# Gated layer's first state turned in 32x32 blocks and exchanged through DRAM; attention as attention @ (h @ W)

## The chip, the cores and the metric

The kernel runs on one core of one Trainium2 chip. The metric is the device time of one execution in microseconds (us). The kernel before was run three times: 3126.87 us is the median, 3125.3 and 3129.24 are the ends. One execution was also taken by the hardware profiler.

## The reference

128 graphs of 128 nodes with 256 features go through four layers, each with a residual: x = x + layer(relu(layernorm(x))). All data are float32. Layers 0 to 2 are graph attentions, cut to what matters here:

```python
Wh = h @ W                                   # (graph, node, 256)
e = (Wh @ a1)[:, :, None] + (Wh @ a2)[:, None, :]
e = jnp.where(e > 0, e, 0.2 * e)
attention = softmax(jnp.where(adj > 0, e, -9e15), axis=-1)
x = x + elu(attention @ Wh)                  # layer 2: times a node mask before elu
```

Layer 3 is a gated graph layer of three steps. Its state begins as h = relu(layernorm(x)). In each step the neighbours are summed, and a GRU cell takes the sum and the state:

```python
aggr = A.T @ (h @ weight[i])
gi, gh = aggr @ w_ih.T + b_ih, h @ w_hh.T + b_hh
r, z = sigmoid(i_r + h_r), sigmoid(i_z + h_z)
n = tanh(i_n + r * h_n)
h = (1 - z) * n + z * h
```

## The kernel before

Four graphs form a group, and 32 groups are worked on. A node is on a partition, so one tile of a group is 128 partitions by 4 graphs by 256 features (`xt`, `xn`, `hn`, `xo`). The GRU works on the transposed form: features on partitions, the 512 nodes of the group along the row, two tiles of 128 features each.

`load` (L67) brings x and the adjacency of a group. `stats` (L170) makes the mean and variance on DVE, and the reciprocal standard deviation `rs` with a power on GpSimd. `attention` (L200) is one attention layer of one group. `xn` is the relu of x minus the mean (ACT); `rs` is a positive number per node, so it is multiplied in later. The scores are not read from h @ W: `VA` holds W @ a1 and W @ a2 spread over all partitions, made once at the start (L84 to L106). DVE makes the first score as a dot product with an accumulator (`scr`, L212), GpSimd multiplies for the second (`pr`, L217) and ACT adds up (L221). TensorE spreads the second score over the partitions by a transpose (`e2`, L229). DVE and ACT make the softmax (`em`, `nmx`, `pe`, L235 to L252). Then TensorE transposes the attention (`atp`, L261), DVE multiplies by `rs` on the way out (`at`), TensorE multiplies it with `xn` (`ahp`, L272), the product is copied to `ah` by ACT and DVE, and TensorE multiplies it with W (`hp`, L285). The elu with the residual is done on ACT (`t`, L291) and DVE (L293, L294) in halves of two graphs, on a tile `xo` that GpSimd filled with x - 1 (L257).

`gat` (L299) runs the three attentions of a group and makes the GRU's first state `hn` (L317). `turned` (L185) transposes it: eight 128x128 transposes on TensorE into PSUM (`hTp`, L191) and two copies (`hT`, L195 and L197). `gru` (L324) does the three steps. Per step, 24 products of 512 columns (L344), four neighbour sums per feature half (`agp`, L361), and from the second step on transposes of the state (`hnp`, L335). At the end the result is added to x and stored.

PSUM has eight banks, given out by tag (L62): two to the attention ("gat"), four to the GRU ("gru"), two to neighbour sums and state transposes ("tr").

The program runs each group's attention two groups ahead of its GRU, and a scheduler of the framework sets the order of instructions on each engine when the kernel is built. Each engine then takes its instructions strictly in this order, and each waits for what it needs. In the order that results, the attention of group g + 1 lies between the GRU products of group g, and the order is the same from group to group in the middle of the run. SP's queue issues all DMAs.

An engine's matmul in float32 is two instructions in the profile.

Of the kernel before, what the change touches and what calls it, by code (L numbers as in the profile page):

```python
# [8 lines left out]
FT = mybir.dt.float32  # L9
I32 = mybir.dt.int32  # L10
AF = mybir.ActivationFunctionType
OP = mybir.AluOpType
AX = mybir.AxisListType

P = 128
# [6 lines left out]
def kernel(  # L22
# [24 lines left out]
    nc = tc.nc  # L47
    B, N, D = x.shape
    KD = D // P
    G = 4  # L50
    NG = B // G
    T = G * N
# [3 lines left out]
    const = ctx.enter_context(tc.tile_pool(name="const", bufs=1))  # L56
# [4 lines left out]
    psum = ctx.enter_context(tc.tile_pool(name="psum", bufs=1, space=bass.MemoryType.PSUM))  # L61
    BANKS = {"gat": 2, "gru": 4, "tr": 2}  # L62

    def bank(tag, name):
        return psum.tile([P, T], FT, tag=tag, name=name, bufs=BANKS[tag])

# [10 lines left out]
    ident = const.tile([P, P], FT, name="ident")  # L77
# [5 lines left out]

    W, VA = [], []  # L84
    for l, (w, a) in enumerate(((w0, a0), (w1, a1), (w2, a2))):
        wt = const.tile([P, KD, D], FT, name=f"w_{l}")
        nc.sync.dma_start(wt, w.rearrange("(k p) o -> p k o", p=P))
        ab = su.tile([P, 2, D], FT, tag="ab", name=f"ab_{l}")
        nc.sync.dma_start(ab, bass.AP(tensor=a.tensor, offset=a.offset, ap=[[0, P], [1, 2 * D]]))
        wa = su.tile([P, 2, KD], FT, tag="wa", name=f"wa_{l}")  # L90
        vp = bank("gat", f"vp_{l}")
        for s in range(2):
            for k in range(KD):
                scr = su.tile([P, D], FT, tag="scr", name=f"scr_{l}_{k}_{s}")
                nc.vector.scalar_tensor_tensor(
                    scr, wt[:, k, :], 1.0, ab[:, s, :], op0=OP.mult, op1=OP.mult,
                    accum_out=wa[:, s, k : k + 1],
                )
                c = s * KD + k
                nc.tensor.transpose(  # L100
                    vp[:, c * P : (c + 1) * P], wa[:, s, k : k + 1].to_broadcast([P, P]), ident
                )
        va = const.tile([P, 2, D], FT, name=f"va_{l}")
        nc.vector.tensor_copy(va.rearrange("p s d -> p (s d)"), vp)
        W.append(wt)
        VA.append(va)  # L106

# [57 lines left out]

    setup.close()
    rw = ctx.enter_context(tc.tile_pool(name="rw", bufs=2))

# [31 lines left out]
    def attention(g, l, xt, cap):  # L200
# [5 lines left out]
        for b in range(G):  # L206
            nc.scalar.activation(xn[:, b, :], xt[:, b, :], AF.Relu, bias=nm[:, b : b + 1])  # L207

        e = gw.tile([P, 2, G], FT, tag="e", name=f"e_{name}")
        for b in range(G):  # L210
            scr = gw.tile([P, D], FT, tag="scr", name=f"scr_{name}_{b}")
            nc.vector.scalar_tensor_tensor(  # L212
                scr, xn[:, b, :], rs[:, b : b + 1], VA[l][:, 0, :], op0=OP.mult, op1=OP.mult,
                accum_out=e[:, 0, b : b + 1],
            )
        pr = gw.tile([P, G, D], FT, tag="pr", name=f"pr_{name}")
        nc.gpsimd.tensor_tensor(  # L217
            pr, xn, VA[l][:, 1 : 2, :].to_broadcast([P, G, D]), op=OP.mult
        )
        for b in range(G):  # L220
            nc.scalar.activation(  # L221
                pr[:, b, :], pr[:, b, :], AF.Copy, scale=rs[:, b : b + 1],
                accum_out=e[:, 1, b : b + 1],
            )
        yield

        e2 = bank("gat", f"e2_{name}")
        for c in range(G):
            nc.tensor.transpose(  # L229
                e2[:, c * P : (c + 1) * P], e[:, 1, c : c + 1].to_broadcast([P, P]), ident  # L230
            )

        em = gw.tile([P, G, N], FT, tag="em", name=f"em_{name}")
        for c in range(G):
            nc.vector.scalar_tensor_tensor(  # L235
                em[:, c, :], e2[:, c * P : (c + 1) * P], e[:, 0, c : c + 1], cap[:, c, :],
                op0=OP.add, op1=OP.min,
            )
# [16 lines left out]

        xo = grp.tile([P, G, D], FT, tag=f"x{l + 1}", name=f"xo_{name}", bufs=3 if l == 2 else 2)
        nc.gpsimd.tensor_scalar(xo, xt, 1.0, -1.0, op0=OP.mult, op1=OP.add)  # L257
        yield
        atp = bank("gat", f"atp_{name}")
        for b in range(G):  # L260
            nc.tensor.transpose(atp[:, b * P : (b + 1) * P], pe[:, b, :], ident)  # L261
        at = gw.tile([P, T], FT, tag="at", name=f"at_{name}")
        nc.vector.tensor_tensor(
            at.rearrange("p (g i) -> p g i", g=G), atp.rearrange("p (g i) -> p g i", g=G),
            rs.rearrange("p (g o) -> p g o", o=1).to_broadcast([P, G, N]), op=OP.mult,
        )

        ah = gw.tile([P, KD, T], FT, tag="ah", name=f"ah_{name}")
        for k in range(KD):
            ps = bank("gat", f"ahp_{name}_{k}")  # L270
            for c in range(G):
                nc.tensor.matmul(  # L272
                    ps[:, c * P : (c + 1) * P], xn[:, c, k * P : (k + 1) * P],
                    at[:, c * P : (c + 1) * P], start=True, stop=True,
                )
            if k % 2 == 0:
                nc.scalar.copy(ah[:, k, :], ps)
            else:
                nc.vector.tensor_copy(ah[:, k, :], ps)  # L279
        for j in range(G // 2):  # L280
            hp = bank("gat", f"hp_{name}_{j}")
            for b in range(2):
                c = 2 * j + b
                for k in range(KD):
                    nc.tensor.matmul(  # L285
                        hp[:, b * D : (b + 1) * D], ah[:, k, c * P : (c + 1) * P], W[l][:, k, :],
                        start=(k == 0), stop=(k == KD - 1),
                    )

            t = gw.tile([P, T], FT, tag="t", name=f"t_{name}_{j}")  # L290
            nc.scalar.activation(t, hp, AF.Exp)  # L291
            u = xo[:, 2 * j : 2 * j + 2, :].rearrange("p b d -> p (b d)")
            nc.vector.scalar_tensor_tensor(u, hp, 0.0, u, op0=OP.max, op1=OP.add)  # L293
            nc.vector.scalar_tensor_tensor(u, t, 1.0, u, op0=OP.min, op1=OP.add)  # L294
        yield xo
# [3 lines left out]
    def gat(g):  # L299
# [16 lines left out]
        for b in range(G):  # L316
            nc.scalar.activation(  # L317
                hn[:, b, :], xt[:, b, :], AF.Relu, bias=nm[:, b : b + 1], scale=rs[:, b : b + 1]
            )
        hT = turned(hn, grp, "h0", f"{g}_3")  # L320
        done[g] = (xt, am, hn, hT)
        yield

    def gru(g):  # L324


        xt, am, hn0, h0 = done.pop(g)
        h = [h0[:, k, :] for k in range(KD)]
        hn = [[hn0[:, b, k * P : (k + 1) * P] for b in range(G)] for k in range(KD)]

        def node_major(i, k):
# [6 lines left out]
            return ps  # L338

        for i in range(STEPS):  # L340
            name = f"{g}_{i}"

            def mm(ps, c, w, v, k, start, stop):
                nc.tensor.matmul(  # L344
                    ps, w[:, k, c * P : (c + 1) * P], v[k], start=start, stop=stop
                )
# [22 lines left out]
            for c in range(KD):  # L369
# [34 lines left out]
                d = rw.tile([P, T], FT, tag="d", name=f"d_{name}_{c}")  # L404
                nc.vector.tensor_sub(d, h[c], n)
                nc.vector.scalar_tensor_tensor(d, z, 1.0, d, op0=OP.add, op1=OP.mult)
# [63 lines left out]
```

## Time and profile before

| what | value |
|---|---|
| median of three runs | 3126.87 us |
| profiled execution, time | 3126.87 us |
| profiled execution, span from first to last instruction | 3125.1 us |
| mean granted TensorE clock | 0.991 |
| TensorE busy before 160 us of the span (two stretches of 80) | 42.13 and 54.62 us |
| TensorE busy, 160 to 300 us | 134.00 of 140 us |
| DMA, share of 16 engines | 4.6% of the span in the one large queue |
| x of a group, 512 KB, issue to landing | 3.9 us |
| result of a group, 512 KB, issue to landing | 2.9 us |
| adjacency of a group, 256 KB | 2.7 us |

The span runs from the first instruction to the last; what lies around it in this execution is 1.8 us. In the first 120 us the weights are prepared and the attention of the first group runs alone, with nothing beside it; that is why TensorE is half idle there. In the lists of groups, a row has the line, the engine, the operation, the tiles and shapes and the count, then the busy time and mean duration of one, then the idle time of the engine just before such instructions, with what ended it. Mean durations of matmuls include their overlap with their neighbours. In a view in order of time, a bracket at the end gives the idle time before the row and what ended it.

### The profile page before, as it was taken

How to read it: one execution, taken by the hardware profiler on the slowest of the kernel's cores; microseconds unless marked ns; L12 is line 12 of the kernel's file. 1: busy time of each engine (PE TensorE's matmuls, PEld its weight loads, DVE VectorE, ACT ScalarE, POOL GpSimd, SP SyncE). 2: the span in 40 equal slices, each digit the busy share in tenths (PEclk: the TensorE clock that was granted, in tenths of full speed). 3: DMA queues.
4: the chain of work that ended last, by engine and by line, in shares of the span. 5: the costliest groups of instructions: out<-in, count | busy, mean ns of one | idle time of the engine just before them, and what ended most of it. 6: DMA issues, size and time to landing. Idle time of an engine off the chain costs nothing.

```text
span 3125.1 us, 32601 instructions
## 1 busy us (share of the span) xinstructions
PE 2941.1 (94%) x11105; PEld 1714.3 (55%) x11105; DVE 2163.8 (69%) x4731; ACT 1349.4 (43%) x3265; POOL 530.0 (17%) x454
## 2 busy tenths in 40 slices
PE   5699999999999999999999999999999999999999
PEld 3455555555555555555555555555555555555554
DVE  5667776767776777776777677677667677767663
ACT  1344444444444444444444444444444444444442
POOL 1212111212111212121112121112121121111110
PEclk8899999999999999999999999999999999999999
DMA  2000000000000000000000000000000000000000
GB/s 85 11 17 11 7 18 17 17 18 11 7 18 17 18 17 11 7 17 18 17 18 11 7 17 18 18 12 13 11 18 17 17 11 7 17 14 7 8 1 14
DMA packets 56199, 48.03 MB, mean 15 GB/s; under 512 B 3296, under 2 KB 55648, under 8 KB 56032
## 3 DMA queue, kind: packets, MB, share of 16 engines
q1 hardware_dynamic: 56032, 45.95, 4.6%
q8 instruction: 87, 1.43, 0.2%
q14 instruction: 80, 0.66, 0.1%
HBM read 29.17 MB, written 16.78 MB: 15 GB/s over the span
## 4 chain that ended last, share of the span: by engine, by line
PE 70%; DVE 13%; ACT 9%; POOL 6%; issue 1%; DMA 0%; ACTq 0%; SPq 0%; POOLq 0%; DVEq 0%
PE r L344 15%; PE z L344 15%; PE ni L344 9%; PE hp L285 7%; PE nn L344 7%; PE ahp L272 6%; POOL pr L217 5%; ACT xn L207 4%; PE agp L361 3%; DVE st L175 3%; DVE xo L294 3%; DVE xo L293 3%; ACT pr L221 2%; PE hnp L335 2%; PE e L229 2%; PE atp L261 2%
## 5 line engine op out<-in xcount | busy, mean ns | idle before, releaser
L212 DVE SCALAR_TENSOR_TENSOR scr<-xn,rs,va 128x256 f32<-128x256 f32 x384 | 386.0, 1053 | 73.0 <-POOL rs L182 71.1
L344 PE MATMUL r<-ag,wc 128*128 128x512 f32 x768 | 372.1, 593 | 0.0
L344 PE MATMUL ni<-ag,wc 128*128 128x512 f32 x768 | 371.4, 592 | 0.0
L285 PE MATMUL hp<-w,ah 128*128 128x256 f32 x1536 | 368.3, 383 | 0.7 <-DVE ah L279 0.7
L344 PE MATMUL z<-ag,wc 128*128 128x512 f32 x768 | 361.4, 592 | 0.0
L257 POOL TENSOR_SCALAR xo<-xo 128x1024 f32<-128x1024 f32 x64 | 67.5, 1055 | 1596.4 <-DVE mv L176 1596.4
L285 PEld LDWEIGHTS hp<-w,ah 128*128 128x128 f32 x1536 | 284.2, 190 | 76.8 <-DVE ah L279 26.3
L293 DVE SCALAR_TENSOR_TENSOR xo<-hp,xo 128x512 f32<-128x512 f32 x192 | 131.0, 683 | 253.6 <-ACT t L291 253.6
L221 ACT ACTIVATE pr<-pr,rs 128x256 f32<-128x256 f32 x384 | 190.4, 496 | 183.5 <-POOL pr L217 183.5
L291 ACT ACTIVATE t<-hp 128x512 f32<-128x512 f32 x192 | 114.7, 597 | 353.5 <-PE hp L285 353.5
L344 PE MATMUL nn<-h,whh 128*128 128x512 f32 x512 | 261.8, 593 | 0.0
L344 PE MATMUL z<-h,whh 128*128 128x512 f32 x512 | 261.5, 592 | 0.0
L344 PE MATMUL r<-h,whh 128*128 128x512 f32 x512 | 261.5, 592 | 0.0
L392 DVE SCALAR_TENSOR_TENSOR n<-r,wn 128x512 f32<-128x512 f32 x192 | 131.4, 685 | 185.2 <-ACT r L390 185.2
L217 POOL TENSOR_TENSOR pr<-xn,va 128x1024 f32<-128x1024 f32 x96 | 236.2, 2461 | 96.6 <-ACT xn L207 96.6
L245 ACT ACTIVATE pe<-em,nmx 128x128 f32<-128x128 f32 x384 | 148.8, 389 | 209.3 <-DVE nmx L241 209.3
L361 PEld LDWEIGHTS agp<-am,hn 128*128 128x128 f32 x1536 | 204.5, 192 | 61.3 <-issue 61.0
L344 PEld LDWEIGHTS z<-ag,wc 128*128 128x128 f32 x768 | 143.3, 190 | 167.5 <-issue 167.4
L397 ACT ACTIVATE n<-n,bi 128x512 f32<-128x512 f32 x192 | 138.3, 720 | 213.1 <-DVE n L396 210.5
L390 ACT ACTIVATE r<-r,brz 128x512 f32<-128x512 f32 x192 | 131.3, 684 | 215.1 <-PE r L344 215.0
L344 PEld LDWEIGHTS ni<-ag,wc 128*128 128x128 f32 x768 | 143.5, 190 | 142.7 <-issue 132.2
L361 PE MATMUL agp<-am,hn 128*128 128x128 f32 x1536 | 218.2, 275 | 0.0
(91 smaller groups left out, 4636.6 us busy)
## 6 DMA issues: line engine op xcount, KB each, us to landing
x<-in_x_dram SPq DMA_DIRECT2D x32, 512.0 KB, 3.9
out_dram<-o SPq DMA_DIRECT2D x32, 512.0 KB, 2.9
adj<-in_adj_dram SPq DMA_DIRECT2D x32, 256.0 KB, 2.7
w<-in_L_gnn_W_dram SPq DMA_DIRECT2D x3, 256.0 KB, 6.9
ab<-in_L_gnn_a_dram SPq DMA_DIRECT2D x3, 256.0 KB, 6.6
whh_ld<-in_L_gnn_w_hh_dram SPq DMA_DIRECT2D x1, 768.0 KB, 8.4
wih_ld<-in_L_gnn_w_ih_dram SPq DMA_DIRECT2D x1, 768.0 KB, 5.9
gt_ld<-in_L_gnn_weight_dram SPq DMA_DIRECT2D x3, 256.0 KB, 2.6
```

The costliest lines, as they stand in the source:

```text
L212: nc.vector.scalar_tensor_tensor(scr, xn[:, b, :], rs[:, b : b + 1], VA[l][:, 0, :], op0=OP.mult, op1=OP.mult, accum_out=e[:, 0, b : b + 1],)
L217: nc.gpsimd.tensor_tensor(pr, xn, VA[l][:, 1 : 2, :].to_broadcast([P, G, D]), op=OP.mult)
L221: nc.scalar.activation(pr[:, b, :], pr[:, b, :], AF.Copy, scale=rs[:, b : b + 1], accum_out=e[:, 1, b : b + 1],)
L245: nc.scalar.activation(pe[:, b, :], em[:, b, :], AF.Exp, bias=nmx[:, b : b + 1], accum_out=sm[:, b : b + 1])
L272: nc.tensor.matmul(ps[:, c * P : (c + 1) * P], xn[:, c, k * P : (k + 1) * P], at[:, c * P : (c + 1) * P], start=True, stop=True,)
L285: nc.tensor.matmul(hp[:, b * D : (b + 1) * D], ah[:, k, c * P : (c + 1) * P], W[l][:, k, :], start=(k == 0), stop=(k == KD - 1),)
L293: nc.vector.scalar_tensor_tensor(u, hp, 0.0, u, op0=OP.max, op1=OP.add)
L344: nc.tensor.matmul(ps, w[:, k, c * P : (c + 1) * P], v[k], start=start, stop=stop)
L361: nc.tensor.matmul(ps[:, b * P : (b + 1) * P], hn[k][b], am[:, b, :], start=True, stop=True)
L390: nc.scalar.activation(r, pr, AF.Tanh, bias=brz[:, cr : cr + 1], scale=0.5)
L392: nc.vector.scalar_tensor_tensor(n, r, 1.0, wn, op0=OP.add, op1=OP.mult)
L397: nc.scalar.activation(n, n, AF.Tanh, bias=bi[:, cn : cn + 1])
```

## The change

It has two parts. In the attention, h @ W is made first, and the attention is multiplied with it; the scores come as two further columns of h @ W. For this W is widened at the start to 258 columns, the last two being W a1 and W a2, and `xn` is transposed by `turned` in each attention. In the gated layer, the first state is no longer transposed by TensorE: DVE transposes it in blocks of 32x32, one DMA writes the result to DRAM and four read it back so that each block lands on its partitions. It then has an order with the 32 columns of a block innermost, and what reads it (`mm`, and the difference in L404 of the new kernel) uses a view of four dimensions. Of the eight PSUM banks the attention now has three and the tag "tr" one.

```diff
-    BANKS = {"gat": 2, "gru": 4, "tr": 2}
+    BANKS = {"gat": 3, "gru": 4, "tr": 1}
+    Q = P // 32
...
-    W, VA = [], []
+    E = D + 2
+    W = []
...
+                scr = su.tile([P, D], FT, tag="scr", name=f"scr_{l}_{k}_{s}")
                 nc.vector.scalar_tensor_tensor(
-                    scr, wt[:, k, :], 1.0, ab[:, s, :], op0=OP.mult, op1=OP.mult,
-                    accum_out=wa[:, s, k : k + 1],
-                )
-                c = s * KD + k
-                nc.tensor.transpose(
-                    vp[:, c * P : (c + 1) * P], wa[:, s, k : k + 1].to_broadcast([P, P]), ident
-                )
+                    scr, wt[:, k, :D], 1.0, ab[:, s, :], op0=OP.mult, op1=OP.mult,
+                    accum_out=wt[:, k, D + s : D + s + 1],
+                )
...
-        e = gw.tile([P, 2, G], FT, tag="e", name=f"e_{name}")
-        for b in range(G):
-            scr = gw.tile([P, D], FT, tag="scr", name=f"scr_{name}_{b}")
-            nc.vector.scalar_tensor_tensor(
-                scr, xn[:, b, :], rs[:, b : b + 1], VA[l][:, 0, :], op0=OP.mult, op1=OP.mult,
-                accum_out=e[:, 0, b : b + 1],
-            )
-        pr = gw.tile([P, G, D], FT, tag="pr", name=f"pr_{name}")
-        nc.gpsimd.tensor_tensor(
-            pr, xn, VA[l][:, 1 : 2, :].to_broadcast([P, G, D]), op=OP.mult
-        )
-        for b in range(G):
-            nc.scalar.activation(
-                pr[:, b, :], pr[:, b, :], AF.Copy, scale=rs[:, b : b + 1],
-                accum_out=e[:, 1, b : b + 1],
-            )
+        hT = turned(xn, gw, "hT", name)
+        yield
+
+        wh = gw.tile([P, G, E], FT, tag="wh", name=f"wh_{name}")
+        for c in range(G):
+            ps = bank("gat", f"whp_{name}_{c}")
+            for k in range(KD):
+                nc.tensor.matmul(
+                    ps[:, :E], hT[:, k, c * P : (c + 1) * P], W[l][:, k, :],
+                    start=(k == 0), stop=(k == KD - 1),
+                )
+            nc.scalar.activation(wh[:, c, :], ps[:, :E], AF.Copy, scale=rs[:, c : c + 1])
         yield
...
-        nc.vector.tensor_tensor(
-            at.rearrange("p (g i) -> p g i", g=G), atp.rearrange("p (g i) -> p g i", g=G),
-            rs.rearrange("p (g o) -> p g o", o=1).to_broadcast([P, G, N]), op=OP.mult,
-        )
-        ah = gw.tile([P, KD, T], FT, tag="ah", name=f"ah_{name}")
-        for k in range(KD):
-            ps = bank("gat", f"ahp_{name}_{k}")
-            for c in range(G):
-                nc.tensor.matmul(
-                    ps[:, c * P : (c + 1) * P], xn[:, c, k * P : (k + 1) * P],
-                    at[:, c * P : (c + 1) * P], start=True, stop=True,
-                )
...
+        nc.vector.tensor_copy(at, atp)
...
-                for k in range(KD):
-                    nc.tensor.matmul(
-                        hp[:, b * D : (b + 1) * D], ah[:, k, c * P : (c + 1) * P], W[l][:, k, :],
-                        start=(k == 0), stop=(k == KD - 1),
-                    )
+                nc.tensor.matmul(
+                    hp[:, b * D : (b + 1) * D], at[:, c * P : (c + 1) * P], wh[:, c, :D],
+                    start=True, stop=True,
+                )
...
-        hT = turned(hn, grp, "h0", f"{g}_3")
+
+        tr = gw.tile([P, Q, KD, G, 32], FT, tag="hT", name=f"tr_{g}_3")
+        for k in range(KD):
+            nc.vector.transpose(
+                tr[:, :, k].rearrange("p j b c -> p b j c"),
+                hn[:, :, k * P : (k + 1) * P].rearrange("p b (j r) -> p b j r", j=Q),
+            )
+        d = dram.tile([Q, 32, Q, KD * G * 32], FT, tag="d", name=f"d_{g}")
+        nc.sync.dma_start(
+            d.rearrange("q r j f -> (q r) j f"), tr.rearrange("p j k b c -> p j (k b c)")
+        )
+        hT = grp.tile([P, Q, KD, G, 32], FT, tag="h0", name=f"h_{g}_0")
+        for j in range(Q):
+            nc.sync.dma_start(
+                hT[j * 32 : (j + 1) * 32].rearrange("p q k b c -> p q (k b c)"),
+                d[:, :, j, :].rearrange("q r f -> r q f"),
+            )
...
-        h = [h0[:, k, :] for k in range(KD)]
+        h = [h0[:, :, k].rearrange("p q b c -> p b q c") for k in range(KD)]
...
+        def like(t, v):
+
+            return t.rearrange("p (b q c) -> p b q c", b=G, q=Q) if len(v.shape) == 4 else t
...
-                    ps, w[:, k, c * P : (c + 1) * P], v[k], start=start, stop=stop
+                    like(ps, v[k]), w[:, k, c * P : (c + 1) * P], v[k], start=start, stop=stop
...
-                nc.vector.tensor_sub(d, h[c], n)
+                nc.vector.tensor_sub(like(d, h[c]), h[c], like(n, h[c]))
```

The residual x - 1 is now in a tile `xm` of its own, and the elu's first half in a tile `u`; their operations stay where they were.

## The prediction

> **What bounds the kernel.** First the busy times by stretch of the span, then the TensorE groups kept apart by shape, then TensorE alone in order of time over one group of four graphs, last all engines around one wait.
>
> ```profile
> PE 2941.1 (94%) x11105; PEld 1714.3 (55%) x11105; DVE 2163.8 (69%) x4731; ACT 1349.4 (43%) x3265; POOL 530.0 (17%) x454
> 300.00:3000.00 2700.00, 2594.65 (x9855) 1513.87 (x9854) 1912.81 (x4170) 1202.39 (x2915) 471.16 (x397) 1.00 0.04 14
> L229 PE MATMUL e<-ident,e 128*128 128x128 f32 x384 | 87.1, 293 | 111.2 <-ACT pr L221 102.4 <-DVE scr L212 8.5
> L191 PE MATMUL hTp<-ident,hn 128*128 128x128 f32 x256 | 55.8, 303 | 29.1 <-ACT hn L317 29.1
> ```
>
> TensorE is busy 2594.65 of the middle 2700 us at full clock: it is the bound, and its 105 us of idle time is what else can be won or lost. Nearly all of that stands before two kinds of transposes: the scores (e) and the last layer's state (hTp).
>
> ```profile
> 1601.31 1.95 PE L272 MATMUL ahp<-at,xn 128*128 128x128 f32 x16
> 1604.87 3.19 PE L285 MATMUL hp<-w,ah 128*128 128x256 f32 x14
> 1607.89 1.02 PE L344 MATMUL r<-h,whh 128*128 128x512 f32 x2
> 1608.75 1.02 PE L344 MATMUL z<-h,whh 128*128 128x512 f32 x2
> 1610.50 0.60 PE L335 MATMUL hnp<-ident,h 128*128 128x128 f32 x4
> 1610.94 1.02 PE L344 MATMUL nn<-h,whh 128*128 128x512 f32 x2
> 1614.64 0.44 PE L191 MATMUL hTp<-ident,hn 128*128 128x128 f32 x2 [0.74 <-ACT hn L317]
> 1658.31 0.32 PE L229 MATMUL e<-ident,e 128*128 128x128 f32 x1 [1.14 <-ACT pr L221]
> 1684.82 0.32 PE L229 MATMUL e<-ident,e 128*128 128x128 f32 x1 [1.49 <-ACT pr L221]
> ```
>
> Columns: start, length, engine, line. Matmuls overlap, so their price is the distance of starts, not the mean length. A GRU product (two instructions) takes 1608.75-1607.89 = 0.86; a 256-wide instruction (1607.89-1604.87)/14 = 0.216; a transpose 0.44/4 = 0.11; the 16 ahp instructions up to the next start at 1603.09 take 1.78, 0.111 each. One group's waits are 0.74+1.14+1.49, and twice 0.17 before a second e transpose: 3.7 us. The first GRU product of successive groups starts at 312.98 and 407.24: 94.3 us a group, which is 90.6 of work and 3.7 of waits.
>
> ```profile
> 1675.40 1.02 PE L344 MATMUL z<-h,whh 128*128 128x512 f32 x2
> 1675.66 0.60 ACT L291 ACTIVATE t<-hp 128x512 f32<-128x512 f32 x1 [1.13 <-PE hp L285]
> 1676.36 0.67 DVE L293 SCALAR_TENSOR_TENSOR xo<-hp,xo 128x512 f32<-128x512 f32 x1
> 1677.35 0.67 DVE L294 SCALAR_TENSOR_TENSOR xo<-t,xo 128x512 f32<-128x512 f32 x1
> 1679.60 0.17 DVE L178 TENSOR_SCALAR nm<-mv 128x4 f32<-128x4 f32 x1
> 1679.81 1.70 ACT L207 ACTIVATE xn<-xo,nm 128x256 f32<-128x256 f32 x4 [3.55 <-DVE nm L178]
> 1681.59 2.54 POOL L217 TENSOR_TENSOR pr<-xn,va 128x1024 f32<-128x1024 f32 x1 [0.58 <-ACT xn L207]
> 1681.86 2.56 DVE L212 SCALAR_TENSOR_TENSOR scr<-xn,rs,va 128x256 f32<-128x256 f32 x1
> ```
>
> From the last hp at 1675.40 it takes 4.4 us until DVE begins nm, 6.1 until ACT has all of xn, then 2.5 for GpSimd's product.
>
> **What the Trainium skill says.** The Trainium skill, "GPSIMD Engine Reference", section 1, Specifications: GpSimd's SBUF interfaces are shared with VectorE, and two-input DVE instructions contend. The trace agrees: scr takes 2.56 us beside pr and 0.48 alone. "PSUM — Partial Sum Buffer", section "PSUM bank collisions raise a hardware error": two engines may not read one bank together. The trace agrees: L293 of the first half starts as L291 on the same hp ends (1674.57 after 1673.94+0.60). "Vector Engine (DVE) Microarchitecture Reference", section 3.8: a 32x32 transpose sustains one element per cycle and lane, no faster than a plain copy; no run here shows it yet. "DMA: Bandwidth & Descriptors", Anatomy of one DMA: about 2 us fixed in each (its fit is for the GpSimd queue); here, from SP, 512 KB lands in 2.9 (out) to 3.9 us (x).
>
> **The change part by part.**
>
> *TensorE's work.* Per attention, ahp goes (-1.78), hp halves from 16 instructions to 8 (-8 x 0.216 = -1.73), the transposes of xn come (8 x 0.11 = +0.88), and xn@[W, W a1, W a2], 16 instructions of 258 columns (16 x 0.218 = +3.49). Net +0.86, times 96 = +82.6. The last layer's 8 transposes go: 32 x 0.88 = -28.2. The 12 setup transposes go: -3. Sum +51 us, 1.6 a group, all on the bound engine.
>
> *Work off TensorE.* DVE loses scr (386+30), ah (66) and the old hT copy (22) and gains 96 copies of hT (0.68 each, 65) and the block transposes (64 x 0.7 = 45): -394. GpSimd loses pr (236), ACT pr (190+72). ACT gains 384 evacuations of 258 columns, between L245 without its accumulator (0.39) and L291 (0.60): 0.46 taken, 177 us; its copy of ah is replaced by one of hT. DVE's copy of at costs what the product at L263 did. None of these is the bound, so I count nothing for totals, only for who is late.
>
> *Which waits go and come.* The waits on pr go: 1.31+1.66 = 3.0 a group. The 0.74 on hn at TensorE goes. But xn@W now starts from transposes of xn on TensorE, so xn itself gates an in-order queue. The order of instructions is the same in all middle groups, so I laid the new queues against durations above. T is the issue of the last hp.
>
> Layer 2: between T and the first xn transpose stand agp (0.89), three GRU products (2.58), a state transpose (0.44) and r (0.86): due at T+4.8, all eight done at T+5.7. Against it: the two halves of hp now issue 0.87 apart instead of 1.75, so DVE's four 512-wide elu steps start at T+0, not T-0.83, and end at T+3.25 instead of T+2.6; one more bn_stats (0.4) now stands behind them. So nm begins at T+5.3, xn starts at T+5.5 and its four quarters (0.43 pitch, 0.2 to be seen) reach TensorE from T+6.1 to T+7.4; transposes end at T+7.75. Wait 2.1. The same stretch hides a second one: the "tr" pool has one PSUM bank now, so state transpose and r wait for DVE's copy of agp, queued behind the statistics, until T+5.3. I add 0.4 for atp and the copy of hT: 2.5.
>
> Layer 1: seven products stand in front, due at T+6.0; xn is behind n's tanh on ACT and starts at T+6.1, so the first quarter comes at T+6.7, the second at T+7.1. Wait 0.9, plus 0.3 for hp, which now has one 0.86 product between it and atp while the copy of at needs about 1.05: 1.2. The scores follow at once: the last 258-wide evacuation ends some 0.7 us after its matmuls, under a product that stands in between.
>
> Boundary (layer 3, and layer 0 of the next group): hn needs GpSimd's rs (1.04), about T+7.0, and n's tanh: it runs from T+7.35 to T+9.45. Queued behind hn on ACT are z's tanh and the copy of the GRU state (0.68+0.59), which agp waits for: due T+9.0, it starts at T+10.8. Wait 1.8. On DVE the two 32x32 transposes wait for hn, and d and h of GRU step 1 are queued behind them; TensorE needs h at T+12.4. At 0.7 each (a plain 512-wide pass) they are just in time; at 1.4 (scattered writes) they add 1.4. I take 0.7, plus 0.4 for small ones: 2.2.
>
> Sum 1.2+2.5+2.2 = 5.9 against 3.7: +2.2 x 31 groups = +68.
>
> *The exchange.* Five DMAs a group on SP: the write waits for DVE's transposes (T+10.9), the next x load stands behind it (needed most of a group later), four reads wait for the write. Write 2.9, reads 3.9, 2 more for sharing with that x load: about T+20. TensorE wants h at T+32, since some 18 us of GRU step 2 lie between: nothing, with 12 us of cover; without it every late microsecond costs 31.
>
> *Step 0's moving operand* is read in runs of 32 floats. Bounds: nothing to 10% of 12 products a group (32 x 10.3 x 0.1 = 33); I take nothing, because element count and type stay.
>
> *Start.* Before the first GRU each layer loses ahp and ah but gains hT and xn@W: about -3 each; the first exchange (about 7) is in the open. -2 in all.
>
> Sum on the profiled execution, 3126.87 (span 3125.1 and 1.8 around it, equal to the median): +51+68-2 = 3244.
>
> **Rivals.**
> - *Waits exchanged one for one* (5.9 is really about 3.7): 3126.9+51-2 = 3176. For it: the new chain has neither the POOL product nor the port contention. Against: nm is later by 0.9-1.1.
> - *Faster.* The only place is the wait before TensorE's attention products: if xn comes as early as the queue expects, removing 3.7 a group (115 us) beats +51. It decides below 2.0 us of waits a group; with 1.0 left, 3126.9+51-84 = 3094. For it: DVE and GpSimd are emptier by 394 and 236 us. Against: 5 us of elu and statistics before xn remain, whose instructions are unchanged.
> - *Worse*: DVE transposes at 1.4 and strided reads slow: 3244+43+33 = 3320. A late exchange would look alike.
> - *It doesn't do what it says*: no; the orders show the transposes, five DMAs and the eight xn transposes in each group.
>
> **Numbers.** Chances: forecast 0.60, one for one 0.20, worse 0.11, faster 0.09. The range 3165 to 3310 takes in the second and most of the third. A measurement can tell 0.2% (6 us) here: faster 0.09, same 0.03, slower 0.88 (the same comes from the one-for-one case at lower waits).
>
> **What would show it.** TensorE idle before hTp (xn) some 3 to 4 us a group, before agp about 2, before e near nothing; instruction starts of whp 0.218 apart; a group period near 98 us; DVE transposes at 0.7; SP's reads landed ten microseconds before nn. If hTp's idle is under 1 us a group, or the period under 94.3, I am wrong.

## The result and the profile after

The changed kernel took 3143.81 us (median of 4 runs, 3142.61 to 3145.15), the kernel before 3128.05 us (4 runs, 3125.3 to 3129.28). The ratio is 1.0052, 95% interval 1.0034 to 1.0069: slower by half a per cent, some 16 us. The forecast was 3244 us. The profiled execution of the changed kernel has a span of 3141.2 us and a time of 3143.79 us, at the same mean clock of 0.991.

The views that carried the forecast, now of the kernel after: busy times of the page, busy times from 300 to 3000 us, and groups over the whole span kept apart by shape (busy time and mean ns of one, then idle time before them and what ended it).

```profile
PE 3017.8 (96%) x10837; PEld 1709.2 (54%) x10837; DVE 1803.2 (57%) x3992; ACT 1298.0 (41%) x2849; POOL 263.1 (8%) x358
...
300.00:3000.00 2700.00, 2644.94 (x9561) 1496.33 (x9560) 1579.91 (x3487) 1149.72 (x2527) 231.04 (x311) 1.00 0.08 25
...
L360 PE MATMUL agp<-am,hn 128*128 128x128 f32 x1536 | 212.9, 278 | 23.1 <-ACT hn L351 16.9 <-ACT hn L296 6.3
L185 PE MATMUL hTp<-ident,xn 128*128 128x128 f32 x768 | 125.5, 284 | 9.6 <-ACT xn L201 9.5
L330 PE MATMUL hnp<-ident,h 128*128 128x128 f32 x768 | 117.1, 275 | 40.1 <-DVE ag L364 37.9 <-DVE h L407 2.2
L218 PE MATMUL e<-ident,wh 128*128 128x128 f32 x384 | 74.9, 277 | 1.2 <-ACT wh L213 0.7
L302 DVE STREAM_TRANSPOSE tr<-hn 128x512 f32<-128x512 f32 x64 | 41.7, 690 | 3.2 <-ACT hn L296 3.2
```

TensorE's busy time in the middle stretch rose from 2594.65 to 2644.94 us, so its idle time fell from 105 to 55 us. Over the whole span before, 111.2 us of idle time stood before e and 29.1 before the state's hTp. Now e has 1.2, and the transposes of xn, where the forecast put its largest waits, have 9.6. What idle time is left stands before hnp (40.1) and agp (23.1).

Stores of successive groups are 94.3 us apart before and 94.9 after, in most groups. That is +0.6 a group, 20 us in 31 groups; the first store comes at 219.16 us in place of 222.75, which gives back 4. So the 16 us are made in the steady state, and one group can be taken apart. I price each row of TensorE by its count times the distance of starts (0.429 us for an instruction of 512 columns, 0.218 for 258, 0.216 for 256 and 0.111 for 128). What a distance between two starts has beyond that price I call late. A group's work and lateness then add up to its period:

| one group, us | work | late | period |
|---|---|---|---|
| before | 89.0 | 5.2 | 94.3 |
| after | 90.75 | 4.15 | 94.9 |
| difference | +1.75 | -1.1 | +0.6 |
| forecast of the difference | +1.6 | +2.2 | +3.8 |

The work is as forecast. The lateness has the wrong sign. The next fences show why, first TensorE of the kernel before, in order of time, around a wait shown in the prediction (the e transpose at 1684.82, with 1.49 of idle time).

```profile
1682.31 1.02 PE L344 MATMUL nn<-h,whh 128*128 128x512 f32 x2
...
1685.31 0.32 PE L229 MATMUL e<-ident,e 128*128 128x128 f32 x1 [0.17 <-ACT pr L221]
1685.47 1.02 PE L344 MATMUL r<-h,whh 128*128 128x512 f32 x2
```

The product at 1682.31 costs 0.86 when the next one follows at once, so e was due at 1683.17. It started at 1684.82: 1.65 late, where the bracket says 1.49. The next transpose costs 0.11 and is followed 0.49 later: 0.38 late, where the bracket says 0.17. A bracket counts from the modelled end of the row before, and that end is later than the point at which the next row could have started: an instruction of 512 columns is listed with 0.59 us and followed after 0.43. Summed like this, the large waits of a group are 1.30+0.38+1.65+0.38 before e, 0.91 before hTp and 0.11 before atp, 4.7 us, and small ones make it 5.2. The forecast added up brackets and had 3.7.

The second view is all engines of the kernel after around layer 2, the place of the largest wait.

```profile
1679.23 1.05 PE L360 MATMUL agp<-am,hn 128*128 128x128 f32 x8
1679.33 0.69 DVE L266 SCALAR_TENSOR_TENSOR u<-hp,xm 128x512 f32<-128x512 f32 x1 [1.39 <-ACT t L264]
...
1680.05 0.69 DVE L270 SCALAR_TENSOR_TENSOR xo<-t,u 128x512 f32<-128x512 f32 x1
...
1680.66 0.68 DVE L266 SCALAR_TENSOR_TENSOR u<-hp,xm 128x512 f32<-128x512 f32 x1
...
1681.26 0.42 DVE L169 BATCH_NORM_STATS2 st<-xo 128x6 f32<-128x256 f32 x1
1681.60 0.67 DVE L270 SCALAR_TENSOR_TENSOR xo<-t,u 128x512 f32<-128x512 f32 x1
1681.84 1.02 PE L343 MATMUL z<-h,whh 128*128 128x512 f32 x2
...
1683.39 0.66 DVE L364 COPY ag<-agp 128x512 f32<-128x512 f32 x1
...
1684.10 0.66 PE L330 MATMUL hnp<-ident,h 128*128 128x128 f32 x4 [1.24 <-DVE ag L364]
1684.17 0.27 DVE L172 TENSOR_SCALAR nm<-mv 128x4 f32<-128x4 f32 x1
1684.47 1.71 ACT L201 ACTIVATE xn<-xo,nm 128x256 f32<-128x256 f32 x4 [2.60 <-DVE nm L172]
...
1685.45 1.32 PE L185 MATMUL hTp<-ident,xn 128*128 128x128 f32 x8
```

T, the point at which the last hp is issued and the next row starts, is 1679.23. On DVE, rows of 0.68 to 0.69 us start 0.60 to 0.61 apart when nothing holds them (1680.05, 1680.66, 1681.26), and the first statistics of 0.42 is followed 0.34 later. So nm starts at T+4.94 (forecast T+5.3) and xn at T+5.24 (T+5.5). But xn is not what TensorE waits for first: hnp needs the one "tr" bank, which DVE's copy ag frees, and ag stands behind the statistics. That is 1.40 us of lateness by distances (1.24 in the bracket). The prediction named this wait, but counted it as hidden inside the wait for xn. When hTp comes, xn is nearly there and costs 0.28 more.

The same view at layer 1 (first fence) and at the boundary (second).

```profile
1655.97 1.02 PE L343 MATMUL ni<-ag,wc 128*128 128x512 f32 x2
...
1660.78 0.17 DVE L172 TENSOR_SCALAR nm<-mv 128x4 f32<-128x4 f32 x1
...
1661.32 1.69 ACT L201 ACTIVATE xn<-xo,nm 128x256 f32<-128x256 f32 x4
...
1661.97 0.72 PE L185 MATMUL hTp<-ident,xn 128*128 128x128 f32 x4
```

```profile
1607.83 1.02 PE L343 MATMUL z<-h,whh 128*128 128x512 f32 x2
...
1614.40 2.08 ACT L296 ACTIVATE hn<-xo,nm,rs 128x256 f32<-128x256 f32 x4
...
1616.51 1.30 DVE L302 STREAM_TRANSPOSE tr<-hn 128x512 f32<-128x512 f32 x2
...
1616.96 0.57 ACT L351 COPY hn<-hnp 128x512 f32<-128x512 f32 x1
...
1617.58 1.16 PE L360 MATMUL agp<-am,hn 128*128 128x128 f32 x8 [0.56 <-ACT hn L351]
...
1617.85 0.34 SPq L307 DMA_DIRECT2D d<-tr  x1
1619.19 0.37 SPq L70 DMA_DIRECT2D x<-in_x_dram  x1
...
1622.39 1.75 SPq L312 DMA_DIRECT2D h<-d  x4
```

In layer 1 (T = 1655.97) xn starts at T+5.35, not T+6.1, and the first transpose starts at T+6.0, exactly when it is due: no wait where 0.9 was forecast. At the boundary (T = 1607.83) hn starts at T+6.57, not T+7.35, and agp at T+9.75, not T+10.8: 0.73 late where 1.8 was forecast. The two DVE transposes take 0.69 each. In this group the write takes 4.5 us to land (the median of the run is 2.7) and the reads 2.6 to 3.1, so h is there at 1626.8; the product that needs it starts at 1639.47, without a wait.

### The profile page after: what moved, and what is told of

Read it like the earlier page. It is cut to its first block, busy times and chain, and to the rows that moved or that the text cites. A ratio compares the mean times of both kernels' runs of the same rounds, so it can differ in the third digit from the quotient of the medians.

```text
span 3141.2 us, 31050 instructions
## 1 busy us (share of the span) xinstructions
PE 3017.8 (96%) x10837; PEld 1709.2 (54%) x10837; DVE 1803.2 (57%) x3992; ACT 1298.0 (41%) x2849; POOL 263.1 (8%) x358
## 4 chain that ended last, share of the span: by engine, by line
PE 77%; DVE 11%; ACT 7%; issue 3%; DMA 1%; POOL 0%; SPq 0%; DVEq 0%; POOLq 0%; ACTq 0%
PE r L343 17%; PE z L343 15%; PE whp L209 11%; PE nn L343 9%; PE ni L343 8%; PE agp L360 5%; PE hp L258 4%; PE hTp L185 3%; DVE st L169 3%; DVE u L266 3%; DVE xo L270 2%; PE hnp L330 2%; ACT pe L234 2%; ACT hn L296 2%; PE atp L250 2%
## 5 line engine op out<-in xcount | busy, mean ns | idle before, releaser
L343 PE MATMUL nn<-h,whh 128*128 128x512 f32 x768 | 394.2, 595 | 1.6 <-DMA h<-d 1.2
L343 PE MATMUL r<-h,whh 128*128 128x512 f32 x768 | 393.2, 594 | 0.0
L343 PE MATMUL z<-h,whh 128*128 128x512 f32 x768 | 392.4, 592 | 0.0
L209 PE MATMUL whp<-w,hT 128*128 128x258 f32 x1536 | 361.1, 384 | 0.8 <-ACT hT L189 0.7
L209 PEld LDWEIGHTS whp<-w,hT 128*128 128x128 f32 x1536 | 288.3, 191 | 88.2 <-ACT hT L189 46.9
L213 ACT ACTIVATE wh<-whp,rs 128x258 f32<-128x258 f32 x384 | 180.0, 477 | 283.7 <-PE whp L209 283.6
L384 ACT ACTIVATE wn<-nn,bh 128x512 f32<-128x512 f32 x192 | 131.3, 684 | 317.6 <-PE nn L343 317.6
L360 PE MATMUL agp<-am,hn 128*128 128x128 f32 x1536 | 212.9, 278 | 23.1 <-ACT hn L351 16.9
L364 DVE COPY ag<-agp 128x512 f32<-128x512 f32 x192 | 130.6, 680 | 172.1 <-PE agp L360 172.1
L343 PEld LDWEIGHTS r<-h,whh 128*128 128x128 f32 x768 | 141.0, 191 | 139.8 <-issue 117.2
L266 DVE SCALAR_TENSOR_TENSOR u<-hp,xm 128x512 f32<-128x512 f32 x192 | 131.8, 687 | 134.5 <-ACT t L264 134.4
```

Source lines behind the costliest of these rows:

```text
L209: nc.tensor.matmul(ps[:, :E], hT[:, k, c * P : (c + 1) * P], W[l][:, k, :], start=(k == 0), stop=(k == KD - 1),)
L213: nc.scalar.activation(wh[:, c, :], ps[:, :E], AF.Copy, scale=rs[:, c : c + 1])
L266: nc.vector.scalar_tensor_tensor(u, hp, 0.0, xm[:, 2 * j : 2 * j + 2, :].rearrange("p b d -> p (b d)"), op0=OP.max, op1=OP.add,)
L343: nc.tensor.matmul(like(ps, v[k]), w[:, k, c * P : (c + 1) * P], v[k], start=start, stop=stop)
L360: nc.tensor.matmul(ps[:, b * P : (b + 1) * P], hn[k][b], am[:, b, :], start=True, stop=True)
L364: nc.vector.tensor_copy(t, ps)
```

## The experiments

Two readings stood against each other. The reading of the trace: the kernel before lost more in front of the scores than was counted, and the new queue, with DVE's rows closer together, loses less; the exchange is hidden and gains a little. Its rivals: the forecast's new waits are real and something else became cheaper; or the exchange made the gain that covers the added work. Where an expectation has letters, A is the reading of the trace. The medians and ratios against the kernel before, which was run again on the same chip. The rows come from several chips, so two rows are compared to within a few us only:

| run | us | ratio (95% interval) | us a group |
|---|---|---|---|
| before | 3128 to 3130 | 1 | 94.3 |
| attention alone | 3159.16 | 1.0095 (1.008 to 1.011) | 95.5 |
| exchange alone | 3121.29 | 0.9968 (0.9955 to 0.998) | 93.5 |
| exchange alone, from the second group on | 3106.94 | 0.9928 (0.9914 to 0.9943) | 93.5 |
| after, first group turned by TensorE | 3140.53 | 1.0037 (1.0024 to 1.005) | 94.9 |
| before without GpSimd's product | 3046.02 | 0.9732 (0.9718 to 0.9747) | 92.0 |
| before without the first score's dot products | 3125.23 | 0.9987 (0.998 to 0.9994) | 94.1 |
| before, both scores on DVE | 3141.52 | 1.0039 (1.0024 to 1.0054) | 93.9 to 95.6 |
| before, GpSimd's product in four | 3194.38 | 1.0206 (1.0189 to 1.0223) | 96.7 |
| that cut and the exchange from the second group on | 3141.58 | 1.004 (1.0025 to 1.0055) | 95.0 |
| after, two banks for "tr" | 3166.73 | 1.0118 (1.0103 to 1.0133) | 95.1 to 96.8 |
| after, transposes of x in place of xn | 3119.62 | 0.997 (0.9958 to 0.9983) | 94.3 |
| after, ag copied by ScalarE | 3139.09 | 1.0034 (1.0021 to 1.0046) | 94.8 |

**The attention alone.** The changed kernel without the exchange.

```diff
-        tr = gw.tile([P, Q, KD, G, 32], FT, tag="hT", name=f"tr_{g}_3")
...
-            )
+        hT = turned(hn, grp, "h0", f"{g}_3")
...
-        h = [h0[:, :, k].rearrange("p q b c -> p b q c") for k in range(KD)]
+        h = [h0[:, k, :] for k in range(KD)]
```

> The attention part alone: the first GRU state is transposed by TensorE again, banks as in the changed kernel. Theory A (TensorE is the clock; an instruction on it costs its distance of starts, and a wait costs what the trace shows before it): against the changed kernel (3144) the eight transposes come back, 32 x 0.88 = +28, a wait on hn of about 0.7 x 31 = +23 comes at them, and the 0.75 us that agp waits behind hn, z and the state copy partly goes, -12: about 3180, so the attention part costs some 50 us and the exchange gives some 40 back. Theory B (the exchange's waits eat what it saves, the attention's work is paid for by waits that go): 3144 or less.

3159.16 us lies between the two theories, so neither number came true: the attention part alone costs about 29 us, 1.3 a group, and the exchange brings 13 to 15 of that back in the changed kernel. A group has 91.6 us of work here, 2.6 more than before, and is 3.9 late, so the attention removes 1.35 of lateness and adds more work than that.

**The exchange alone**, in the kernel before.

```diff
-        hT = turned(hn, grp, "h0", f"{g}_3")
+        tr = gw.tile([P, Q, KD, G, 32], FT, tag="hT", name=f"tr_{g}_3")
...
-        h = [h0[:, k, :] for k in range(KD)]
+        h = [h0[:, :, k].rearrange("p q b c -> p b q c") for k in range(KD)]
```

> The exchange alone, on the attention and the banks of the kernel before. Theory A: 28 us of transposes and the 0.74 us wait on hn (23 us) go, a wait of some 0.7 us for agp behind hn comes (-51+22): about 3100, faster than both kernels. Theory B: waits take the place, about 3128. A third way: the scores' waits move with the new order and the time falls anywhere between 3080 and 3140.

3121.29 us, a smaller gain than the 3100 that the reading gave; only the wide third range holds it. TensorE's groups in the middle stretch say what took its place: z products that wait for DVE, which has the two transposes on its queue.

```profile
L366 PE MATMUL z<-h,whh 128*128 128x512 f32 x692 | 356.4, 597 | 17.4 <-DVE n L418 17.4
...
L232 PE MATMUL e<-ident,e 128*128 128x128 f32 x344 | 75.9, 289 | 84.8 <-ACT pr L224 84.8
```

By distances of starts, hTp's 0.89 of work and 1.1 of lateness went, 0.86 came back before z and 0.33 before r, and e's wait stayed: 0.8 a group is gained. The rest is the start: the first store comes at 243.38 us in place of 222.75, because the first GRU product now stands in TensorE's queue behind the second group's attention and begins at 142.22 us, not at 121.09.

**The exchange from the second group on.** The same, with the first group's state turned by TensorE.

```diff
+        if g == 0:
+            hT = turned(hn, grp, "h0", f"{g}_3")
+        else:
+            tr = gw.tile([P, Q, KD, G, 32], FT, tag="hT", name=f"tr_{g}_3")
```

> The exchange on the attention of before, but the first group's state is transposed on TensorE. Reading: the stores of the exchange alone run at 93.5 us a group against 94.3 before, and its first store comes 20.6 us later than before, since the first GRU product stands behind group 1's attention in TensorE's queue; with the first group on TensorE this goes, and the time is 3098 to 3106. If the late start has another cause, it stays at 3121.

3106.94 us, a little above the forecast 3098 to 3106: some 13 us of start are gone, with the same 93.5 a group. It is the fastest version here that computes everything, and beats both kernels.

**The same in the changed kernel.** The edit is that of the diff above.

> The changed kernel with only the first group's state transposed on TensorE; all later groups by the exchange. If the first exchange costs the changed kernel only what the trace shows before the first GRU product (1.2 us on the reads and some 3.4 on the chain behind), 3138 to 3142. If it costs what it cost when the exchange was added alone (12 to 20 us), 3124 to 3132.

3140.53 us, in the first range: in the changed kernel the first exchange costs some 3 us only, which is less than the two intervals can tell apart. There the first GRU product begins at 122.83 us with the exchange and at 115.82 without it, a delay of 7 us where it was 18 in the other pair (142.22 and 123.96), since it was not put behind a whole attention; the first store comes 4.3 us later.

**Without GpSimd's product.** ACT's sums read xn directly, so the second score's weights are left out.

```diff
-        nc.gpsimd.tensor_tensor(
-            pr, xn, VA[l][:, 1 : 2, :].to_broadcast([P, G, D]), op=OP.mult
-        )
...
-                pr[:, b, :], pr[:, b, :], AF.Copy, scale=rs[:, b : b + 1],
+                pr[:, b, :], xn[:, b, :], AF.Copy, scale=rs[:, b : b + 1],
```

> The kernel before without GpSimd's product for the second score: ACT adds up xn itself, so that part of the score is left out; ACT and DVE do as much as before. Theory A: the 3.0 us a group that TensorE waits for the scores come from this product (2.46 us, and it slows DVE's dot products from 0.48 to 2.56 us), which the built order takes for shorter; without it nearly all of 31 x 3.0 = 93 us go: 3035 to 3060. Theory E: the wait comes from ACT's eight instructions behind it, and stays in good part: 3090 to 3128.

3046.02 us, 84 less, in the first range. The row of e over the whole span:

```profile
L226 PE MATMUL e<-ident,e 128*128 128x128 f32 x384 | 77.6, 281 | 15.1 <-ACT pr L218 6.2 <-DVE scr L212 5.9
```

111.2 us of idle time before e became 15.1, nearly all of it before the middle stretch. A group takes 92.0 us, which is the same 89.0 of work and 2.9 late, in place of 5.2. Of the 3.7 us of lateness before e 3.5 went, and 1.2 came back before ahp, r and hTp. 2.3 x 31 is 71 us; the rest of the 84 lies in the start, where nothing hides the product: the first store comes 11.6 us sooner. So most of the lateness before the scores can be won as time, and about a third of it turns up elsewhere.

**Without the first score's dot products** on DVE; the first score is left out.

```diff
-            nc.vector.scalar_tensor_tensor(
-                scr, xn[:, b, :], rs[:, b : b + 1], VA[l][:, 0, :], op0=OP.mult, op1=OP.mult,
-                accum_out=e[:, 0, b : b + 1],
-            )
+            nc.vector.tensor_copy(e[:, 0, b : b + 1], rs[:, b : b + 1])
```

> The kernel before without DVE's dot products for the first score (that part of the score is left out), GpSimd's product and ACT's sums kept. If the 3 us a group of waits before the scores come from the length of the product itself (2.46 us, which the built order takes for shorter), they stay: 3115 to 3130. If they come from the port that DVE and GpSimd share, the product gets shorter without DVE beside it and the waits go: 3040 to 3070.

3125.23 us, in the first range and 4 us from the kernel before, next to nothing. GpSimd's product takes 2402 ns beside no dot product, 2462 beside them, and e waits as before. Of the contention that the prediction speaks of, VectorE pays nearly all (its dot product of 2.56 us) and GpSimd 60 ns: the wait is the product's own length and the four sums behind it.

**Both scores on DVE**, the second one first.

```diff
+                scr, xn[:, b, :], rs[:, b : b + 1], VA[l][:, 1, :], op0=OP.mult, op1=OP.mult,
+                accum_out=e[:, 1, b : b + 1],
+            )
+        for b in range(G):
...
                 scr, xn[:, b, :], rs[:, b : b + 1], VA[l][:, 0, :], op0=OP.mult, op1=OP.mult,
                 accum_out=e[:, 0, b : b + 1],
...
-        nc.gpsimd.tensor_tensor(
-            pr, xn, VA[l][:, 1 : 2, :].to_broadcast([P, G, D]), op=OP.mult
-        )
```

> The kernel before with both scores as dot products on DVE, second score first, and no product on GpSimd nor sums on ACT; the whole result is computed. DVE: 8 instructions of some 0.48 and 0.08 us an attention instead of four of 1.05: about the same busy time, 430 us. If the product on GpSimd is what the scores wait for, this gives what its removal gave: 3045 to 3070. If DVE becomes late instead (elu and statistics queue behind the second four), 3080 to 3130.

3141.52 us, no gain, outside both ranges: e still waits, now for DVE (0.98 and 0.79 of idle time in a group). Behind 20 of the 28 such pairs of waits after the start the clock was halved for more than 3 us, and the two products after them lost 0.8 each; those groups take 95.6 us, the others 93.9.

**GpSimd's product in four**, so that ACT can begin after a quarter; then the same with the exchange from the second group on.

```diff
-        nc.gpsimd.tensor_tensor(
-            pr, xn, VA[l][:, 1 : 2, :].to_broadcast([P, G, D]), op=OP.mult
-        )
+        for b in range(G):
+            nc.gpsimd.tensor_tensor(pr[:, b, :], xn[:, b, :], VA[l][:, 1, :], op=OP.mult)
```

> The kernel before, with GpSimd's product for the second score cut into four products of one graph each, so that ACT can add up each as it comes. Nothing is left out. If the waits of 3.0 us a group before the score transposes come from the row of one long product and four sums behind it: the last sum now ends some 0.5 us after the last product instead of 2.0, so 1.3 to 1.5 us of each of the two waits go, 2.6 to 2.9 a group: 3128 - 31 x 2.7 = 3044, with the price of three more GpSimd starts in each product 3040 to 3075. If the length of GpSimd's work alone decides, no less than 3100.

> The same cut together with the exchange from the second group on (the exchange alone gave 3107). If both gains stand in different places they add: 3107 - 31 x 2.7 = 3023, with the price of the GpSimd starts 3020 to 3055. If the exchange's gain was made by moving waits that the cut takes away anyway, 3045 to 3080.

3194.38 and 3141.58 us: the gains that were expected missed by far in both. The other case of the first, that the length of GpSimd's work alone decides and the time is no less than 3100, has the right range, but it did not foresee a loss. Groups of the first of the two in the middle stretch, on GpSimd and on TensorE:

```profile
L218 POOL TENSOR_TENSOR pr<-xn,va 128x256 f32<-128x256 f32 x332 | 271.8, 844 | 11.8 <-ACT xn L207 11.8
...
L343 PE MATMUL r<-ag,wc 128*128 128x512 f32 x668 | 334.5, 601 | 39.8 <-DVE ag L364 39.8
...
L228 PE MATMUL e<-ident,e 128*128 128x128 f32 x336 | 84.9, 294 | 55.5 <-ACT pr L220 55.5
```

A product of a quarter takes 844 ns, four of them 3.4 us where one of the whole took 2.46. So the last quarter is done later, what ACT gains behind it is mostly eaten, and e keeps 55.5 of the 84.5 us of idle time that it has in this stretch before. The larger loss is in the order: in the queue that was built here, DVE's copy ag stands behind all four dot products of layer 0, which now run 0.9 apart beside GpSimd's longer work, and r waits 1.47 for it in each group. A quarter costs 0.23 us more than a quarter of the whole (844 less 2462/4); no run separates a fixed cost of each instruction from contention in it.

**Two banks for "tr"** in the changed kernel, and two for the attention.

```diff
-    BANKS = {"gat": 3, "gru": 4, "tr": 1}
+    BANKS = {"gat": 2, "gru": 4, "tr": 2}
```

> The changed kernel with two banks for neighbour sums and state transposes again, and two instead of three for the attention. Theory A: the 1.24 us that the state transpose waits for DVE's copy of the sum in layer 2 (38 us in all) is due to the single bank and goes; two banks suffice for h @ W, since the evacuation (0.48 and some 0.35 of hand-over) is as long as the 0.87 of a product: about 3110. Rival C: the products of h @ W now wait for their evacuation at each of the last two banks, 0.2 to 0.4 us an attention, and the time is 3120 to 3150. Rival D: the wait is due to DVE's order (the copy stands behind the statistics), r waits there anyway, and nothing changes: 3144.

3166.73 us, slower, and none of the three cases. hnp's wait is gone, and one before ni took its place. TensorE in order of time at the boundary of two successive groups, then the busy time of the engines in a stretch after each of the two waits (PE, PEld, DVE, ACT, POOL), with the granted clock behind it:

```profile
1537.07 1.12 PE L343 MATMUL ni<-ag,wc 128*128 128x512 f32 x2 [1.90 <-DVE ag L364]
1538.03 0.60 PE L330 MATMUL hnp<-ident,h 128*128 128x128 f32 x4
...
1629.23 1.05 PE L360 MATMUL agp<-am,hn 128*128 128x128 f32 x8
1632.18 1.57 PE L343 MATMUL ni<-ag,wc 128*128 128x512 f32 x2 [1.89 <-DVE ag L364]
1633.55 1.06 PE L330 MATMUL hnp<-ident,h 128*128 128x128 f32 x4
1634.40 1.89 PE L343 MATMUL nn<-h,whh 128*128 128x512 f32 x2
1636.11 1.04 PE L343 MATMUL r<-h,whh 128*128 128x512 f32 x2
```

```profile
1537.00:1541.00 4.00, 3.93 (x12) 2.02 (x13) 2.85 (x9) 2.18 (x6) 1.15 (x2) 1.00 0.32 131
1632.00:1636.00 4.00, 3.82 (x8) 2.00 (x9) 2.96 (x9) 0.89 (x2) 1.04 (x2) 0.59 0.31 124
```

After the second of these waits the mean clock is 0.59 over 4 us (0.50 from 1633 to 1636): ni takes 1.37 in place of 0.86, hnp 0.85 in place of 0.44, nn 1.71 in place of 0.86, 1.8 us in all. After the first, just as long, the clock stays full and ni is followed by hnp after 0.96. The wait stands in 30 groups; the clock fell behind 8 of them, whose period is 96.8 in place of 95.1. That makes some 13 of the 23 us that this run is slower than the changed kernel; some 6 lie in the start, where the first store comes later, and the rest in 0.2 a group.

**Transposes of x in place of xn**, so that they wait for no norm; the norm and relu in front of h @ W are left out.

```diff
-        hT = turned(xn, gw, "hT", name)
+        hT = turned(xt, gw, "hT", name)
```

> The changed kernel with TensorE's transposes in the attention reading x instead of xn, so the norm and relu before h @ W are left out there (xn is still made); everything else of the changed kernel stays. The transposes can start 2 us earlier in each attention. Reading of the trace (xn hardly gates TensorE: at most 0.4 us a group in front of or within hTp): 12 us at most come off, 3130 to 3145. My forecast's chain (2 to 3 us a group of waits on xn): 60 to 90 us come off, 3055 to 3085.

3119.62 us: 24 less than after, below the reading's range and far above what the forecast's chain of 2 to 3 us a group on xn would have given. Neither case came true. Groups in the middle stretch:

```profile
L209 PE MATMUL whp<-w,hT 128*128 128x258 f32 x1392 | 339.7, 386 | 9.9 <-ACT wh L213 9.9
...
L218 PE MATMUL e<-ident,wh 128*128 128x128 f32 x348 | 72.0, 281 | 23.6 <-ACT wh L213 23.6
```

The wait on ag at hnp went in the order built here, and 0.8 us of idle time before e and 0.3 before whp came, on ACT's evacuations. So xn's own wait is not shown alone by this run.

**ag copied by ScalarE** in the changed kernel, away from the statistics on DVE.

```diff
-                nc.vector.tensor_copy(t, ps)
+                nc.scalar.copy(t, ps)
```

> The changed kernel with the copy of the neighbour sums (ag, from agp) made by ScalarE in place of VectorE, so that it no longer stands behind the statistics in VectorE's queue. Nothing is left out. If the largest wait that is left in the changed kernel, 1.24 us of idle and 1.40 by the distance of starts before hnp in each group, comes from that place in VectorE's queue and nothing takes its place: 3144 - 31 x 1.4 = 3100, 3095 to 3115. If ScalarE, which has two tanh and four xn in the same stretch and already makes agp late at the boundary, only takes the wait over: 3130 to 3165.

3139.09 us, in the rival's range: 5 less than after, not 43, and within the two intervals no difference at all. Groups of TensorE in the middle stretch:

```profile
L360 PE MATMUL agp<-am,hn 128*128 128x128 f32 x1360 | 182.1, 277 | 41.4 <-ACT hn L351 41.4
...
L185 PE MATMUL hTp<-ident,xn 128*128 128x128 f32 x682 | 107.5, 277 | 22.5 <-ACT xn L201 22.5
```

hnp's wait is gone. In a group of this run hTp in layer 2 is 0.96 late for xn, which stood right behind, and agp at the boundary 1.62 for ACT's longer queue, in place of 0.73. This run shows the wait for xn that the forecast took for the main one: it is there, at less than half the 2.1 us forecast, and in the changed kernel hidden by ag's.

One more thing holds xn back. With ag gone from DVE's queue, nm starts sooner, at T+4.41 (T is 1677.29 here), but xn starts at T+5.23, as in the changed kernel (T+5.24):

```profile
1681.42 1.04 POOL L246 TENSOR_SCALAR xm<-x 128x1024 f32<-128x1024 f32 x1
1681.70 0.79 DVE L172 TENSOR_SCALAR nm<-mv 128x4 f32<-128x4 f32 x1
1682.52 1.71 ACT L201 ACTIVATE xn<-xo,nm 128x256 f32<-128x256 f32 x4 [2.12 <-DVE nm L172]
```

The small nm lasts 0.79 us beside GpSimd's fill of xm, where it lasts 0.17 with no fill beside it, and it ends 0.03 after the fill. So it is in layer 2 of every group in the middle of this run. No run here moves the fill away, so that it holds nm is not shown by an experiment.

## Why the prediction was wrong

*The direction and the work were right.* TensorE's work was put at +1.6 us a group and measured +1.75.

*The step that failed is the balance of waits, "5.9 against 3.7: +2.2 x 31 groups = +68".* Measured by one yardstick, it is 4.15 against 5.2, or -1.1 in place of +2.2. Both sides are wrong, and their errors add.

The side of before, 3.7, was the sum of idle times in brackets; by distances of starts it is 5.2, 1.5 more a group or 46 us. The sum could have shown it: 94.3 less 3.7 was called "90.6 of work", a remainder, while count times price gives 89.0. The run without GpSimd's product shows that 2.3 us of this lateness can be won as time.

The side of after, 5.9, is 1.75 too large, 54 us. By its terms, each counted from its T to the next: layer 1, 1.2 forecast and 0.4 measured, because xn comes at T+5.35, not T+6.1; boundary, 2.2 forecast and 1.5 measured, because hn and agp start 0.8 and 1.05 earlier; layer 2, 2.5 forecast and 2.25 measured, but of other make: 1.40 for ag at hnp and 0.28 at hTp, where 2.1 for xn was forecast. The likely cause in the first two, and in xn, is that DVE's queue was laid out with durations of 0.67 to 0.69 for rows that start 0.60 apart, though the prediction used distances of starts for TensorE: the four elu steps were put at an end of T+3.25 and end at T+3.04, and nm at T+5.3 and starts at T+4.94. Over a chain of a dozen rows, with what stands behind it, the lead is 0.3 to 0.8 us. This is read from the traces; no run isolates it. The Trainium skill, "Perfetto Trace Analysis", section Optimizing Scalar/DVE Operations, says that in the profiled time of a DVE instruction the write-acknowledgement half of its access overhead overlaps with the next instruction; the trace agrees that they overlap, by 0.08 us on rows of 0.69.

Together 46 and 54 us are the 100 us between the forecast and the result; the other terms leave about nothing. The prediction's own sign of being wrong came: hTp's idle time is 9.6 us over the span, 0.3 a group, where 3 to 4 were forecast.

*The exchange in the middle was right*: hidden, with some 12 us to spare, and nothing seen from reading in runs of 32 floats (an nn instruction means 595 ns over all steps, 593 before). DVE's transposes were taken at 0.7 and measured 0.69, as long as the copy ag of the same width (0.68). What the exchange gains in the changed kernel, 95.5 to 94.9 a group, is less than the 0.88 of work that it removes.

*The start* was put at -2 and is -4 with the end. In the changed kernel the first exchange costs 3 us; alone in the kernel before it costs some 13, by its place in TensorE's queue.

*The rivals.* "One for one" (3176) was nearest, and half of its argument holds: the waits behind GpSimd's product went with the product. The contention, its other half, hardly made them, as the run without the dot products shows. The gain in lateness went beyond it. That a point of balance lies at 2.0 us of waits a group, below which the change would gain, came from the same 3.7: with 5.2 it lies at 5.2 - 1.75, about 3.5, and the measured 4.15 is not far above.

What stays open: why single runs fell so often outside the times expected of them, that is, how much of the gains and losses of single edits comes from the new order that the scheduler builds with each. The run with a cut product shows that this part can be the larger one. Open too are small delays among the products r on ag, 0.4 us a group in the changed kernel and with the exchange alone, 0.06 before.

## What to carry to other kernels

Before a wait is weighed against another, measure both in the same way: count times the distance of starts for every row of a period, the rest is late, and the sum must give the period. Lay out every in-order engine by distances of starts, not only the one that bounds. When a wait is taken away, ask which wait stands right behind it: here ag hid xn, and moving ag brought 5 us at most of a possible 43.

## What was not expected of the hardware

The TensorE clock was halved for more than 3 us behind short idle times, but not behind all of them: with two banks for "tr" behind 8 of 30 waits of 1.89 us, and with both scores on DVE behind 20 of 28 pairs of waits of 0.98 and 0.79. Behind the 30 waits of 1.49 us in the kernel before it stayed full. The Trainium skill, "TensorE: Matmul & The Clock Gate", section "HAM oscillation — how this bites in real kernels", gives idle gaps of more than some 3.4 us as what to avoid; here shorter ones were at times enough, and no run shows what decides.

GpSimd's product of 1024 elements a partition takes 2.40 us without DVE's dot products and 2.46 beside them, and four of 256 take 0.84 each.
